# Moving transfers, merging softmax sums and shortening the tail in a two-layer attention kernel

## The chip, the cores and the metric

The kernel runs on one core of a Trainium2 chip. The metric is the device time of one execution in microseconds (us); a kernel is run several times, and medians are quoted with the lowest and highest run beside them. "Span" is the length of the one execution that was profiled; it lies some 2 us below the time of the same run. The *granted clock* is the share of TensorE's full clock that the profile records; in these traces it is 1.00 or 0.5 at any moment, and a stretch can have a mean between. TensorE is called PE in the profile, VectorE is DVE, ScalarE is ACT, GpSimd is POOL, and SP is the engine that issues most of the transfers.

## The reference

Eight images of 64 channels and 64 x 64 pixels go through two attention layers. Both have 4096 tokens per image and a softmax over all of them; layer 0 has 8 channels for f and g, layer 1 has 64 for q and k and a group norm ahead.

```
def layer0(x, Wf, bf, Wg, bg, Wh, bh):
    xf = x.reshape(b, c, n)
    f = einsum('oc,bcn->bon', Wf, xf) + bf
    g = einsum('oc,bcn->bon', Wg, xf) + bg
    hh = einsum('oc,bcn->bon', Wh, xf) + bh
    beta = softmax(einsum('bci,bcj->bij', f, g), axis=2)
    return x + einsum('bcj,bij->bci', hh, beta)

def layer1(x, gamma, beta, w_qkv, b_qkv, w_proj, b_proj):
    xn = group_norm(x, gamma, beta)
    q, k, v = split(einsum('oc,bchw->bohw', w_qkv, xn) + b_qkv)
    attn = softmax(q @ k.T * c ** -0.5)
    out = einsum('oc,bchw->bohw', w_proj, attn @ v) + b_proj
    return out + x
# x: (8, 64, 64, 64) fp32; output = layer1(layer0(x))
```

## The kernel before

The work is cut into 64 *chunks*: 8 images x 2 layers x 4 groups of queries. A chunk has 16 *steps*; in each, PE makes scores, ACT takes the exponential into tiles `e`, PE multiplies these by the values into an accumulator `acc`, and DVE adds the tiles into `esum`, from which the softmax sums come. The order of the layers is L0 of image 0, L0 of image 1, L1 of image 0, L0 of image 2, L1 of image 1, and so on; so L1 of image 6 is chunks 56 to 59 and L1 of image 7 chunks 60 to 63. Work that prepares the next layer or finishes the last chunk hangs in a list with a step number (`at_step`) and is put between the steps when its number is due. A layer's preparation is numbered from the start of a block of 64 steps.

The end of a chunk, with the four narrow products of ones that sum `esum` over the partitions, and a trip through DRAM that spreads the reciprocals over the partitions:

```
        def finish(self, acc, esum, c, index):
            raw = work.tile([P, CW], F32, tag="raw", ...)
            self.total(raw, acc)                       # empties the accumulators
            ...
            def sums(spare):
                ...
                for p in range(2):
                    for h in range(2):
                        matmul(z[ts(2 * h + p, 32), :], ones, esum[:, p, h, :],
                               start=True, stop=True, tile_position=(0, 32 * (2 * h + p)))
                zs = work.tile([P, CW], F32, tag="zs", ...)
                nc.scalar.copy(zs, z)
                for h in range(2):
                    for p in range(2):
                        row = 32 * (2 * h + p)
                        nc.sync.dma_start(zt[ts(h, C), p, :], zs[row : row + 1, :])

            def reciprocals():
                nc.vector.tensor_add(zh, zt[:, 0, :], zt[:, 1, :])
                rt = stash[:, ts(index, QP)]
                nc.vector.reciprocal(rt, zh)
                nc.sync.dma_start(dealt, rt)
                for h in range(2):
                    row = dealt[ts(h, C), :].rearrange("p e -> (p e)")
                    nc.sync.dma_start(r[ts(h, C), :], row.partition_broadcast(C))

            def result():
                nc.vector.tensor_mul(raw, raw, r)
                self.residual(raw, c)
```

Layer 0's preparation: two projections, each of which ends in 16 small transfers that deal f and g to the partitions:

```
            return [(5, begin, True), (8, lambda: self.project(1), True)] + [ ... values ... ]

        def project(self, k):
            ...
            high = work.tile([P, 2, CW], F32R, tag="high", bufs=1, ...)
            ...
            for j in range(2):
                ...   # 8 transfers for each j
                nc.sync.dma_start(dst[rows, cols].bitcast(F32), split[...].bitcast(F32))
```

Layer 1's preparation (group statistics, normalised input, projections), the numbering of a chunk's end, and the last lines: the check of all reciprocals against bounds makes a flag `n_bad`, on which every engine then branches to a general path that is never taken here.

```
            at = [13, 17, 21]
            units = [(at[0], channels, False), (at[1], means, True), (at[2], deviations, True)]
            for c in range(NC):
                s = 30 + 8 * c
                units += [(s - 5, lambda c=c: normal(c), False), ...]
...
            at_step(now + delay, lambda: sums(spare), not spare)
            at_step(now + delay + 2, reciprocals, False)
            at_step(now + delay + 4, result, False)
...
    while later:
        later.pop(0)[2]()
    ok = work.tile(list(stash.shape), F32, tag="zs", name="ok")
    ...                                            # bounds check of all 64 x 8 columns
    nc.vector.tensor_copy(n_bad, ps[0:1, 0, 0:1])
```

## Time and profile before

| | before |
|---|---|
| time, median of the first 3 runs (us) | 3171.41 (3170.2 to 3171.55) |
| span of the profiled run (us) | 3168.3 |
| PE / DVE / ACT busy | 98% / 78% / 65% |
| first exp of the first chunk (us) | 22.40 |
| last accumulation to the end of the span (us) | 18.90 |

How to read it: PE is busy nearly all the time, so only what PE does or waits for can move the time much. The table of waits of the kernel before gives what waited, for what, in total, how often and at the longest (us). The wait that the argument is about is small in it:

```profile
PE acc_l L123 <- DVE raw_l L529: 10.9, 6, 2.3
```

Six waits, one in each of the six chunks in which layer 1's second chunk runs beside the next image's preparation.

In the rest of the document I use one table that is my own working from the traces: the length of each of the 64 chunks, from its first exp instruction to the first of the next (the last one to the end of the span). It adds up to the span together with the *head*, the time before the first exp.

### The profile page before, as it was taken

The page shows a single profiled execution, that of the slowest core. Times are in us where ns is not written, and L with a number is a line of the kernel's source. Part 1 is how long each engine was busy: PE and PEld are TensorE (multiplying, and loading weights), DVE is VectorE, ACT ScalarE, POOL GpSimd, SP SyncE. Part 2 cuts the span into 40 slices and gives each one's busy share as a digit, 9 for nine tenths or more (in the row PEclk, how much of TensorE's full clock was granted, in tenths as well). Part 3 has the DMA queues.
Part 4 walks back from the last instruction along what each step waited for, and adds up shares of the span by engine and source line. Part 5 has one row for each costly group of instructions (what it writes and reads, how often), then busy time and mean ns, then how long its engine had stood idle before and what let it go on. Part 6 is the DMA issues. An engine that isn't in the chain of part 4 may idle for free.

```text
span 3168.3 us, 58576 instructions
## 1 busy us (share of the span) xinstructions
PE 3102.1 (98%) x25525; PEld 1144.6 (36%) x25525; DVE 2467.3 (78%) x1620; ACT 2068.7 (65%) x2225; POOL 16.6 (1%) x41
## 2 busy tenths in 40 slices
PE   7999999999999999999999999999999999999997
PEld 2333334433343333433334333443333433333432
DVE  6999776797768977689776897768977699766675
ACT  5787655786557865578655786557855588555554
POOL 2000000000000000000000000000000000000000
PEclk9999999999999999999999999999999999999999
DMA  4000010100101010010100101001010000000000
GB/s 95 8 8 18 21 28 15 31 8 22 24 15 31 8 29 17 18 28 8 35 11 18 28 8 34 12 18 28 11 31 20 10 18 8 5 21 15 12 11 16
DMA packets 66409, 63.54 MB, mean 20 GB/s; under 512 B 39409, under 2 KB 39489, under 8 KB 66145
## 3 DMA queue, kind: packets, MB, share of 16 engines
q1 hardware_dynamic: 65024, 59.56, 7.8%
q8 instruction: 202, 3.31, 0.4%
q14 instruction: 63, 0.51, 0.1%
q0 software_dynamic: 800, 0.15, 0.0%
q10 hardware_dynamic: 320, 0.01, 0.0%
HBM read 25.33 MB, written 8.65 MB: 11 GB/s over the span
## 4 chain that ended last, share of the span: by engine, by line
PE 86%; DVE 6%; ACT 3%; DMA 2%; SPq 2%; issue 1%; ACTq 0%; DVEq 0%
PE acc_l L123 51%; PE s_l L123 30%; DVE esum_l L602 4%; ACT e_l L630 3%; PE z_l L123 2%; SPq L390 1%; PE qk_l L123 1%; PE v_l L123 1%; DMA r_l<-recips 1%; DVE high_l L380 0%; DMA zt_l<-zs_l 0%; SPq L312 0%; DMA recips<-stash 0%; PE fg_l L123 0%; DMA w<-in_WgT_dram 0%
## 5 line engine op out<-in xcount | busy, mean ns | idle before, releaser
L630 ACT ACTIVATE e_l<-s_l 128x1024 f32<-128x1024 f32 x2048 | 1968.5, 1025 | 1056.2 <-PE s_l L123 1056.2
L602 DVE TENSOR_TENSOR esum_l<-esum_l,e_l 128x2048 f32<-128x2048 f32 x896 | 2050.3, 2288 | 399.6 <-ACT e_l L630 356.8
L123 PE MATMUL acc_l<-e_l,v_l 64*64 64x512 f32 (+1 forms) x8704 | 1126.7, 593 | 10.9 <-DVE raw_l L529 10.9
L123 PE MATMUL s_l<-kq_l 64*64 64x512 f32 (+1 forms) x8448 | 1035.1, 587 | 6.7 <-DVE v_l L282 4.7
L123 PE MATMUL acc_l<-e_l,vt_l 128*64 128x512 f32 x3584 | 838.9, 602 | 0.7
L123 PEld LDWEIGHTS acc_l<-e_l,v_l 64*64 64x64 f32 (+1 forms) x8704 | 384.6, 134 | 578.6 <-issue 516.3
L123 PEld LDWEIGHTS s_l<-kq_l 64*64 64x64 f32 (+1 forms) x8448 | 375.7, 135 | 574.8 <-issue 524.8
L123 PEld LDWEIGHTS acc_l<-e_l,vt_l 128*64 128x64 f32 x3584 | 229.8, 136 | 458.8 <-issue 447.3
L123 PE MATMUL s_l<-fg_l 32*128 32x512 f32 x1792 | 230.8, 469 | 16.0 <-ACT e_l L630 9.8
L123 PEld LDWEIGHTS s_l<-fg_l 32*128 32x128 f32 x1792 | 92.4, 183 | 277.9 <-ACT e_l L630 194.3
L602 DVE TENSOR_TENSOR esum_l<-e_l,e_l 128x2048 f32<-128x2048 f32 x64 | 146.2, 2285 | 47.2 <-ACT e_l L630 47.2
L326 DVE TENSOR_TENSOR raw_l<-raw_l,r_l 128x512 f32<-128x512 f32 x64 | 44.1, 689 | 82.1 <-DMA r_l<-recips 81.9
L316 DVE TENSOR_TENSOR zh_l<-zt_l 128x8 f32<-128x8 f32 x64 | 10.5, 164 | 101.8 <-DMA zt_l<-zs_l 101.8
L123 PE MATMUL z_l<-esum_l,ones 128*32 128x512 f32 x512 | 68.2, 604 | 1.5 <-DVE vt_l L282 1.4
L529 DVE COPY raw_l<-acc_l 128x512 f32<-128x512 f32 x32 | 22.1, 690 | 28.8 <-PE acc_l L123 28.8
L308 ACT COPY zs_l<-z_l 128x512 f32<-128x512 f32 x64 | 38.2, 598 | 5.0 <-PE z_l L123 5.0
L503 ACT ACTIVATE kq_l<-qk_l,qkb 128x512 f32<-128x512 f32 x64 | 40.6, 696 | 0.0
L123 PE MATMUL qk_l<-xn_l,wqk 64*64 64x512 f32 x256 | 33.9, 592 | 0.0
L282 DVE COPY v_l<-v_l 128x512 f32<-128x512 f32 x36 | 24.7, 687 | 6.9 <-PE v_l L123 6.9
L123 PEld LDWEIGHTS v_l<-wh,x 64*64 64x64 f32 x1024 | 22.9, 140 | 14.8 <-issue 13.1
L123 PE MATMUL fg_l<-x,wfg 64*64 64x512 f32 x128 | 18.3, 652 | 9.7 <-DVE low L165 9.7
L123 PEld LDWEIGHTS v_l<-wvp,xn_l 64*64 64x64 f32 x1024 | 21.5, 134 | 16.0 <-issue 14.5
(83 smaller groups left out, 345.2 us busy)
## 6 DMA issues: line engine op xcount, KB each, us to landing
r_l<-recips SPq DMA_DIRECT2D x128, 128.0 KB, 2.9
fg_l<-high_l SPq DMA_DIRECT2D x224, 64.0 KB, 2.0
x<-in_x_dram SPq DMA_DIRECT2D x32, 256.0 KB, 4.8
kq_l<-kq_l SPq DMA_DIRECT2D x64, 128.0 KB, 2.3
out_dram<-raw_l SPq DMA_DIRECT2D x64, 128.0 KB, 2.3
zt_l<-zs_l SPq DMA_DIRECT2D x256, 2.0 KB, 1.8
kq_l<-high_l SPq DMA_DIRECT2D x32, 64.0 KB, 2.0
recips<-stash SPq DMA_DIRECT2D x64, 4.0 KB, 1.4
```

Of the source, the lines that this page charges most:

```text
L123: in_order(nc.tensor.matmul(*args, **kwargs))
L282: self.copy_values(self.vt[:, :, ts(c, TPC), :], ps[:, :, 0 : TPC * C].rearrange("k p (t c) -> k p t c", c=C),)
L308: nc.scalar.copy(zs, z)
L316: nc.vector.tensor_add(zh, zt[:, 0, :], zt[:, 1, :])
L326: nc.vector.tensor_mul(raw, raw, r)
L390: nc.sync.dma_start(dst[rows, cols].bitcast(F32), split[ts(2 * j + i, 32), half, :].bitcast(F32),)
L503: nc.scalar.activation(self.parts[:, h, cols], ps[:, h, :], AF.Identity, bias=k1["qkb"][:, h : h + 1],)
L529: nc.vector.tensor_copy(raw, acc[0])
L602: nc.vector.tensor_add(esum, first if t == 1 else esum, e)
L630: nc.scalar.activation(e[:, p], ps, AF.Exp, scale=at.scale)
```

## The change

Its intent: five things. (1) In layer 1 DVE adds the two halves of `esum`, so the products of ones have 256 columns instead of 512. (2) Work that ends in transfers is numbered so that the 16 f/g transfers and the transfers of the sums do not meet: layer 0's projections go from steps 5 and 8 to 2 and 25, reciprocals come 3 or 4 steps after the sums instead of 2 and results as long again after them, and layer 1's statistics come 3 steps and its normalising 2 steps later. (3) The last chunk takes its reciprocals of the full 128x512 sums straight from PSUM, without the transfers, and its bounds are checked apart. (4) Images 1 and 2 are loaded behind image 0's 32 f/g transfers, and (5) image 1's projections start at steps 12 and 28.

```diff
@@ finish
-            self.total(raw, acc)
+            copied = self.total(raw, acc)
+            width = CW if self.kind == 0 else CW // 2
+            if self.kind == 1:
+                with tc.issue_after(copied.ins):
+                    nc.vector.tensor_add(esum[:, 0], esum[:, 0], esum[:, 1])
 ...
+                        what = esum[:, i, h, :] if self.kind == 0 else esum[:, 0, h, ts(i, width)]
                         matmul(
-                            z[ts(2 * h + p, 32), :], ones, esum[:, p, h, :],
-                            start=True, stop=True, tile_position=(0, 32 * (2 * h + p)),
+                            z[row : row + 32, 0:width], ones[:, 0:32], what,
+                            start=True, stop=True, tile_position=(0, row),
                         )
 ...
+            def at_once():
+                z = ps_s.tile([P, 2, CW], F32, tag="s", name=f"z_{n}")[:, 0, :]
+                for h in range(2):
+                    matmul(z[ts(h, C), :], ones, esum[:, 0, h, :], start=True, stop=True)
+                nc.vector.reciprocal(r, z)
+                result()
+                bounds(r, 1)
 ...
+            if index == 2 * B * NC - 1:
+                return (at_once,)
@@ Layer0.before
-            return [(5, begin, True), (8, lambda: self.project(1), True)] + [
+            at = (12, 28) if self.b == 1 else (2, 25)
+            return [(at[0], begin, True), (at[1], lambda: self.project(1), True)] + [
@@ Layer1.before
-            at = [13, 17, 21]
+            at = [16, 20, 24]
 ...
-                    (s - 5, lambda c=c: normal(c), False),
+                    (s - 3, lambda c=c: normal(c), False),
@@ start
-    for b in (1, 2):
-        load_x(b)
+    with tc.issue_after(layers0[0].sent.ins):
+        for b in (1, 2):
+            load_x(b)
@@ weigh
-            at_step(now + delay + 2, reciprocals, False)
-            at_step(now + delay + 4, result, False)
+            wait = 4 if i + 1 < len(seq) and seq[i + 1][0].kind == 0 else 3
+            at_step(now + delay + wait, reciprocals, False)
+            at_step(now + delay + 2 * wait, result, False)
@@ end
+    bounds(stash, 0)
     while later:
         later.pop(0)[2]()
 ...
-    matmul(ps[0:1, 0, 0:1], bad, ones[:, 0:1], start=True, stop=True)
-    nc.vector.tensor_copy(n_bad, ps[0:1, 0, 0:1])
+    matmul(bad_ps, bad[:, 0:1], ones[:, 0:1], start=True, stop=False)
+    matmul(bad_ps, bad[:, 1:2], ones[:, 0:1], start=False, stop=True)
+    nc.vector.tensor_copy(n_bad, bad_ps)
```

More of the change, by code (lines that the diff above doesn't have):

```diff
@@ L62 @@
     fast_path(tc, n_bad, *args)
-    reg = nc.values_load(n_bad[0:1, 0:1], min_val=0, max_val=P)
+    reg = nc.values_load(n_bad[0:1, 0:1], min_val=0, max_val=2 * P)
     with tc.If(reg > 0):
@@ L178, in fast_path @@
     make_identity(nc, ident)
-    ones = const.tile([P, 32], F32, name="ones")
+    ones = const.tile([P, C], F32, name="ones")
     nc.vector.memset(ones, 1.0)
@@ L198, in fast_path @@
     QP = 2 * CW // P
-    stash = const.tile([P, 2 * B * NC * QP], F32, name="stash")
+    stash = const.tile([P, (2 * B * NC - 1) * QP], F32, name="stash")
     recips = [dram.tile([P, QP], F32, name=f"recips_{i}") for i in range(2 * B * NC)]
@@ L300, in sums @@
                     z = ps_s.tile([P, 2, CW], F32, tag="s", name=f"z_{n}")[:, 0, :]
-                for p in range(2):
-                    for h in range(2):
+                zs = work.tile([P, CW], F32, tag="zs", name=f"zs_{n}")[:, 0:width]
+                for h in range(2):
+                    for i in range(2):
+                        row = 32 * (2 * h + i)
+                        what = esum[:, i, h, :] if self.kind == 0 else esum[:, 0, h, ts(i, width)]
                         matmul(
-                            z[ts(2 * h + p, 32), :], ones, esum[:, p, h, :],
-                            start=True, stop=True, tile_position=(0, 32 * (2 * h + p)),
-                        )
-                zs = work.tile([P, CW], F32, tag="zs", name=f"zs_{n}")
-                nc.scalar.copy(zs, z)
+                            z[row : row + 32, 0:width], ones[:, 0:32], what,
+                            start=True, stop=True, tile_position=(0, row),
+                        )
+                nc.scalar.copy(zs, z[:, 0:width])
                 for h in range(2):
-                    for p in range(2):
-                        row = 32 * (2 * h + p)
-                        nc.sync.dma_start(zt[ts(h, C), p, :], zs[row : row + 1, :])
+                    for i in range(2):
+                        row = 32 * (2 * h + i)
+                        dst = zt[ts(h, C), i, :] if self.kind == 0 else zt[row : row + 32, 0, :]
+                        nc.sync.dma_start(dst, zs[row : row + 1, :])
             def reciprocals():
-                zh = small.tile([P, QP], F32, tag="zh", name=f"zh_{n}")
-                nc.vector.tensor_add(zh, zt[:, 0, :], zt[:, 1, :])
+                zh = zt[:, 0, :]
+                if self.kind == 0:
+                    nc.vector.tensor_add(zh, zh, zt[:, 1, :])
                 rt = stash[:, ts(index, QP)]
@@ L323, in reciprocals @@
                     nc.sync.dma_start(r[ts(h, C), :], row.partition_broadcast(C))
+            def at_once():
+                z = ps_s.tile([P, 2, CW], F32, tag="s", name=f"z_{n}")[:, 0, :]
+                for h in range(2):
+                    matmul(z[ts(h, C), :], ones, esum[:, 0, h, :], start=True, stop=True)
+                nc.vector.reciprocal(r, z)
+                result()
+                bounds(r, 1)
             def result():
@@ L389, in project @@
                         for i, (dst, half) in enumerate(((self.f, h), (self.g, p))):
-                            nc.sync.dma_start(
+                            self.sent = nc.sync.dma_start(
                                 dst[rows, cols].bitcast(F32),
@@ L529, in total @@
             nc.vector.tensor_copy(raw, acc[0])
-            nc.vector.tensor_add(raw, acc[1], raw)
+            return nc.vector.tensor_add(raw, acc[1], raw)
         def residual(self, o, c):
@@ L608, in weigh @@
                 delay = NT
-            sums, reciprocals, result = at.finish(acc, esum, c, i)
+            works = at.finish(acc, esum, c, i)
+            if len(works) == 1:
+                at_step(now, works[0])
+                return
+            sums, reciprocals, result = works
             at_step(now + delay, lambda: sums(spare), not spare)
-            at_step(now + delay + 2, reciprocals, False)
-            at_step(now + delay + 4, result, False)
+            wait = 4 if i + 1 < len(seq) and seq[i + 1][0].kind == 0 else 3
+            at_step(now + delay + wait, reciprocals, False)
+            at_step(now + delay + 2 * wait, result, False)
     for i, (at, c) in enumerate(seq):
@@ L640, in fast_path, with bounds @@
         weigh(*r, len(seq) * NT)
+    bad = const.tile([P, 2], F32, name="bad")
+    bad_ps = ps_a.tile([P, CW], F32, tag="a", name="bad_ps")[0:1, 0:1]
+    def bounds(recip, i):
+        ok = work.tile(list(recip.shape), F32, tag="zs", name=f"ok_{i}")
+        nc.vector.tensor_scalar(ok, recip, 1.0 / SUM_MAX, None, op0=ALU.is_ge)
+        nc.vector.scalar_tensor_tensor(
+            ok, recip, 1.0 / SUM_MIN, ok, op0=ALU.is_le, op1=ALU.mult
+        )
+        least = small.tile([P, 1], F32, tag="least", name=f"least_{i}")
+        nc.vector.tensor_reduce(least, ok, axis=AX.X, op=ALU.min)
+        nc.vector.tensor_scalar(bad[:, i : i + 1], least, -1.0, 1.0, op0=ALU.mult, op1=ALU.add)
+    bounds(stash, 0)
     while later:
         later.pop(0)[2]()
-    ok = work.tile(list(stash.shape), F32, tag="zs", name="ok")
-    nc.vector.tensor_scalar(ok, stash, 1.0 / SUM_MAX, None, op0=ALU.is_ge)
-    nc.vector.scalar_tensor_tensor(ok, stash, 1.0 / SUM_MIN, ok, op0=ALU.is_le, op1=ALU.mult)
-    least = small.tile([P, 1], F32, tag="least", name="least")
-    nc.vector.tensor_reduce(least, ok, axis=AX.X, op=ALU.min)
-    bad = small.tile([P, 1], F32, tag="bad", name="bad")
-    nc.vector.tensor_scalar(bad, least, -1.0, 1.0, op0=ALU.mult, op1=ALU.add)
-    ps = ps_s.tile([P, 2, CW], F32, tag="s", name="bad_ps")
-    matmul(ps[0:1, 0, 0:1], bad, ones[:, 0:1], start=True, stop=True)
-    nc.vector.tensor_copy(n_bad, ps[0:1, 0, 0:1])
+    matmul(bad_ps, bad[:, 0:1], ones[:, 0:1], start=True, stop=False)
+    matmul(bad_ps, bad[:, 1:2], ones[:, 0:1], start=False, stop=True)
+    nc.vector.tensor_copy(n_bad, bad_ps)
 @with_exitstack
```

## The prediction

> **What bounds the kernel now.** I read the page first, for the engines' shares.
>
> ```profile
> PE 3102.1 (98%) x25525; PEld 1144.6 (36%) x25525; DVE 2467.3 (78%) x1620; ACT 2068.7 (65%) x2225; POOL 16.6 (1%) x41
> PEclk9999999999999999999999999999999999999999
> L326 DVE TENSOR_TENSOR raw_l<-raw_l,r_l 128x512 f32<-128x512 f32 x64 | 44.1, 689 | 82.1 <-DMA r_l<-recips 81.9
> L316 DVE TENSOR_TENSOR zh_l<-zt_l 128x8 f32<-128x8 f32 x64 | 10.5, 164 | 101.8 <-DMA zt_l<-zs_l 101.8
> L123 PE MATMUL z_l<-esum_l,ones 128*32 128x512 f32 x512 | 68.2, 604 | 1.5 <-DVE vt_l L282 1.4
> ```
>
> TensorE (PE) is busy 98% of 3168.3 us, at a granted clock above nine tenths. VectorE (DVE) sits 184 us before two instructions, waiting for the transfers that carry the softmax sums (zt) and the reciprocals (r). That is no gain in itself: PE idles only 66 us in all, and 184 us of DVE waiting can cost no more than what of it reaches PE.
>
> So I cut the span into 64 chunks of 32 exp instructions on ACT (one chunk is 512 queries of one image and layer) and compared chunks of the same kind with the view of stretches. The first row is layer 1's second chunk of image 1, beside which the next image's layer 0 is prepared; the second is the same chunk of image 6, with no layer 0 beside it; the third is a bare chunk of the last image.
>
> ```profile
> core 0: us, PE busy (x) PEld busy (x) DVE busy (x) ACT busy (x) POOL busy (x), PEclk, DMA share, GB/s
> 803.36:865.46 62.10, 60.41 (x536) 23.34 (x532) 45.77 (x45) 32.67 (x35) 0.00 (x0) 0.97 0.06 14
> 2747.45:2805.34 57.89, 57.89 (x536) 20.35 (x532) 41.51 (x43) 32.70 (x35) 0.00 (x0) 1.00 0.07 15
> 2980.08:3036.25 56.17, 56.17 (x524) 22.01 (x520) 37.36 (x22) 31.55 (x34) 0.00 (x0) 1.00 0.04 11
> ```
>
> The first two rows have the same 536 PE instructions, yet differ by 4.2 us: 1.7 us idle, the rest slowed matmuls, which count as busy. The timelines of the DMA queue (SP), DVE and PE just before show why:
>
> ```profile
> 768.97 10.67 SPq L390 DMA_DIRECT2D fg_l<-high_l  x16
> 779.74 2.46 SPq L312 DMA_DIRECT2D zt_l<-zs_l  x4
> ```
>
> ```profile
> 783.40 0.17 DVE L316 TENSOR_TENSOR zh_l<-zt_l 128x8 f32<-128x8 f32 x1 [8.63 <-DMA zt_l<-zs_l]
> 792.32 16.60 DVE L602 TENSOR_TENSOR esum_l<-esum_l,e_l 128x2048 f32<-128x2048 f32 x7
> 808.85 0.68 DVE L529 COPY raw_l<-acc_l 128x512 f32<-128x512 f32 x1
> ```
>
> ```profile
> 809.59 3.62 PE L123 MATMUL acc_l<-e_l,v_l 64*64 64x512 f32 x14 [1.69 <-DVE raw_l L529]
> ```
>
> Sixteen f/g transfers hold the queue for 10.67 us, the sums' transfers wait behind them, DVE waits 8.63 us for those, works off seven exp sums in one piece, and empties the accumulators too late, for which PE waits. Against the undisturbed 57.9 us, the six chunks of this kind took 61.94, 62.10, 60.75, 62.00, 61.03 and 60.26: 20.7 us lost together. The chain of waits shows the two ends of the span; at the start the weights land late among x transfers, at the end three transfers in a row stand between the sums and the result:
>
> ```profile
> 2.70 6.46 DMA w<-in_WgT_dram
> ...
> 3153.12 1.79 DMA zt_l<-zs_l
> ...
> 3155.46 1.39 DMA recips<-stash
> ...
> 3157.42 3.29 DMA r_l<-recips
> ```
>
> [...] The trace has only 8-column reciprocals, 203 ns against about 153 ns for one-column one-source operations: 50 ns for 7 columns, or 7 ns a column. It does not contradict a slow reciprocal.
>
> **The change part by part.**
>
> 1. *Merged sums, 256-column products.* In layer 1, for 31 of 32 chunks, DVE adds the halves of esum[...] and loses the 0.16 us add of zh. The ones products keep eight instructions, four at a time, so two rounds: 2 x 0.43 become 2 x 0.21 us. A bare chunk (56.17 us) is 32 blocks of 1.717 us (54.94) plus 1.23 for the product; it should become 55.75. PE is the bound there, so this is on the path: 31 x 0.43 = 13.3 us; I take 12.5[...]. [...] DVE has some 19 us of slack a chunk, behind the emptying of the accumulators, so off the path.
> 2. *Placement.* Layer 0's two projections move from steps 5 and 8 to 2 and 25 of the 64 (a step is 3.4 us in layer 1); sums of the chunk before come at 7, reciprocals 3 or 4 steps later instead of 2. Sixteen issues from step 3 end at about 6, ahead of the sums. The wait of 8.63 us should vanish, and with it most of the 20.7 us; I take 16.5 (80%), since the second projection (2.0 us of DVE) now falls beside the normalising work of steps 24 to 30.
> 3. *Early chunks and image 6.* Chunks 5 to 7, image 1's layer 0 with layer 1's preparation, took 40.2, 45.6 and 42.8 us against 38.0 for a plain one; they hold 3.2 us of PE waiting for a copy of v. The last preparation holds 1.6. I take 3.5 and 1.5: some of it is real work.
> 4. *Images 1, 2 behind f and g.* The last weights wait 6.46 us to land, in a stretch where x transfers of 256 KB land 1.1 us apart; with four of them ahead instead of nine, I take 1.7 us earlier start. Image 1's projections at 12 and 28 also leave the first chunk (45.4 us, 6 above its work) more room: 3 us more with chunks 0 to 2.
> 5. *The end.* From the last accumulation (3149.44) to the end are 18.9 us. After: copy and add 1.45,[...] products of two 64-column halves about 1.1, reciprocal of 128x512 by 7 ns a column 3.6 plus fixed 0.15, product and residual 1.5; then output to the end as now, 6.0 (3162.3 to 3168.3). Sum 15.0, so 3.9 gained. Were the reciprocal as fast as an add, 0.7 us, it would be 7.
>
> Sum: 12.5 + 16.5 + 3.5 + 1.5 + 1.7 + 3 + 3.9 = 42.6 us, so 3171.4 - 42.6 = 3129 us.
>
> **The rivals.**
>
> *The wait moves.* [...] the projection at 25, the deviations at 24, results at 27 and the merge could together delay a copy of v, and PE waits for its buffer. For it: DVE is busiest in this very chunk (45.8 of 62 us)[...]. Against: 58 us of room. It would give back 1 to 2 us an image: about 3140.
>
> *DVE becomes the bound in layer 0.* A plain layer 0 chunk lasts 38.0 us with 36.4 to 36.8 of DVE. For it: margin of about a microsecond. Against: the merge of the last layer 1 chunk falls into layer 0's first chunk, where DVE has 4 us free, and nothing is added to the other three. If it bites, 7 images lose 1 us each.
>
> *The transfers were hidden anyway.* If the 20.7 us came from the order of PE's work rather than the late DVE, placement gives nothing: 3145. Against: equal instructions, 57.9 us where no f/g transfer runs.
>
> *The end gives nothing.* A slow reciprocal on 512 columns, and bounds checks queued ahead of it: 2 to 4 us.
>
> **Range and chances.** All parts at their full size (13.3, 20.7, 8 in the early chunks, 7 at the end) give some 3115; placement failing by half together with a small end gives 3145. What is left is PE work that the change does not touch, so over 2% (below 3108) would need gains that I see nowhere: 6%. Slower by over 2% would need a new stall of 1.6 us in every chunk: 1%.
>
> **What would show it.** The z group with 256 columns for most and about half the duration; bare chunks at about 55.7 us; waits of DVE for zt and r at a third or less of 184 us; PE's wait for raw gone, and the six chunks near 57.5 plus the moved projection (1 us); first exp at about 20.7 instead of 22.4 us; a reciprocal of 3 to 4.5 us at the end and the end some 15 us behind the last accumulation. I would be wrong if a 256-column product cost as much as one of 512 (the switch, not the columns, being its price), if PE waited elsewhere for DVE, or if image 1 came too late at step 12.

Passages that rested on something that no trace or run of this case shows are cut from it; the cuts are marked. The sum came to 42.6 us and 3129 us with all its terms. One term of part 5 went with the cuts, the time of the merge on DVE: the terms that are left there add up to 13.8 us (1.45 + 1.1 + 3.6 + 0.15 + 1.5 + 6.0), while the 15.0 us and the 3.9 us gained have the merge in them. In part 1, what DVE's merges would cost is cut too, and so is the ground for taking 12.5 us instead of 13.3, which was not shown. That 256 columns should take half of 512's 0.43 us was an estimate from that figure.

## The result and the profile after

The changed kernel took 3135.51 us (3133.82 to 3137.1, 5 runs), the kernel before 3171.55 us (3170.2 to 3175.55, 5 runs) on the same chip. All outputs are right. The ratio is 0.9885, with a 95% interval of 0.9872 to 0.9899: faster by 1.15%, which counts as the same at the 2% mark. (A ratio is the mean time of one kernel's fast runs over the mean of the other's from the same rounds, so it is not quite the ratio of the medians.) Predicted were 3129 us and a gain of 42.6 us; measured is a gain of 36.0 us in the medians and of 34.5 us in the spans.

Rows of the page after that answer to those in the prediction (its span is 3133.8 us):

```profile
PE 3082.4 (98%) x25523; PEld 1145.6 (37%) x25523; DVE 2505.2 (80%) x1624; ACT 2061.3 (66%) x2224; POOL 16.5 (1%) x41
L344 DVE TENSOR_TENSOR raw_l<-raw_l,r_l 128x512 f32<-128x512 f32 x64 | 44.1, 689 | 80.0 <-DMA r_l<-recips 79.9
L327 DVE RECIPROCAL stash<-zt_l 128x8 f32<-128x8 f32 x63 | 12.7, 202 | 42.4 <-DMA zt_l<-zs_l 41.4
L296 DVE TENSOR_TENSOR esum_l<-esum_l 128x1024 f32<-128x1024 f32 x32 | 38.9, 1215 | 0.0
```

PE is still the bound at 98%. DVE does more (38.9 us of merging, the last row, 1215 ns each), and it still waits for transfers: 79.9 us for r as before, and 41.4 us for zt, to which 13.0 us before layer 0's remaining add of zt come. That is 134 us, where I had expected a third of 184 us or less.

The groups by form show the narrower products (mean ns is the number behind the busy time):

```profile
L123 PE MATMUL z_l<-esum_l,ones 128*32 128x512 f32 x256 | 34.1, 605 | 0.0
L123 PE MATMUL z_l<-esum_l,ones 128*32 128x256 f32 x248 | 19.8, 391 | 1.3 <-DVE vt_l L282 1.3
L123 PE MATMUL z_l<-esum_l,ones 128*64 128x512 f32 x4 | 2.0, 1081 | 2.8 <-DVE esum_l L296 2.8
```

248 of the products, 8 in each of 31 chunks, now have 256 columns. Their means, 605 and 391 ns, include the time in which four overlap (by the starts in the traces, in a bare chunk the second four begin 0.45 us behind the first with 512 columns, in the kernel before, and 0.24 us with 256, in the kernel after), so the mean fell by a third only; what counts is the chunk.

Stretches of three chunks after, in the columns of the prediction's stretches (length, then busy time and number of instructions of PE, PE weight loads, DVE, ACT and POOL, then granted clock, DMA share and GB/s): layer 1's second chunk of image 1, of image 6, and a bare chunk of image 7.

```profile
795.39:854.03 58.64, 58.64 (x544) 22.32 (x540) 44.19 (x45) 33.56 (x37) 0.00 (x0) 1.00 0.13 33
2716.68:2775.55 58.87, 57.77 (x536) 22.02 (x532) 42.38 (x43) 32.55 (x35) 0.00 (x0) 1.00 0.07 15
2948.22:3003.97 55.75, 55.75 (x524) 22.03 (x520) 38.36 (x22) 31.31 (x34) 0.00 (x0) 1.00 0.04 11
```

The first went from 62.10 to 58.64 us although it took in eight PE instructions, and PE has no gap in it any more; the wait of PE for raw is no longer in the table of waits. The bare one is the predicted 55.75. The second, with no layer 0 near it, grew by about 1 us and has a gap of 1.10 us that was not there.

The timelines of SP and DVE ahead of the first of these chunks show the transfers apart: the 16 f/g transfers are done before the four of the sums are issued.

```profile
751.56 10.43 SPq L412 DMA_DIRECT2D fg_l<-high_l  x16
765.84 2.42 SPq L320 DMA_DIRECT2D zt_l<-zs_l  x4
```

```profile
769.47 0.17 DVE L325 TENSOR_TENSOR zt_l<-zt_l 128x8 f32<-128x8 f32 x1 [1.80 <-DMA zt_l<-zs_l]
...
797.94 0.69 DVE L551 COPY raw_l<-acc_l 128x512 f32<-128x512 f32 x1 [1.71 <-PE acc_l L123]
```

The wait for zt fell from 8.63 to 1.80 us. And at the second line the roles are exchanged: DVE now stands ready and waits 1.71 us for PE's accumulator, where before PE waited 1.69 us for DVE's copy.

By chunks (sums in us, my working from the traces):

| part of the span | before | after | gain | of which merged sums, 0.43 a chunk |
|---|---|---|---|---|
| head, to the first exp | 22.40 | 21.49 | 0.9 | |
| chunks 0 to 2 | 128.67 | 128.77 | -0.1 | |
| chunks 5 to 7 | 128.55 | 127.30 | 1.3 | |
| layer 1, images 0 to 5, first chunks | 348.71 | 343.56 | 5.2 | |
| same, second chunks | 368.07 | 352.49 | 15.6 | 2.6 |
| same, third chunks | 366.30 | 363.66 | 2.6 | 2.6 |
| layer 0, images 2 to 7 (chunks 12 to 55) | 914.20 | 908.91 | 5.3 | 5.2 |
| image 6 (chunks 56 to 59) | 232.87 | 232.21 | 0.7 | 1.3 |
| bare chunks 60 to 62 | 168.50 | 167.22 | 1.3 | 1.3 |
| last chunk with the end | 75.86 | 74.11 | 1.8 | 0.4 |

The rows gain 34.4 us; the spans differ by 34.5. Layer 1's fourth chunks are 338.24 us in both. So merged sums are 13.3 us, placement 5.2 + 15.6 - 2.6 = 18.2 us, and everything else together about 2.8 us, where I had put 13.6.

### The profile page after: what moved, and what is told of

Same layout as the page of the kernel before. It is cut to its first block, busy times and chain, and to the rows that moved or that the text cites. A ratio compares the mean times of both kernels' runs of the same rounds, so it can differ in the third digit from the quotient of the medians.

```text
span 3133.8 us, 58576 instructions
## 1 busy us (share of the span) xinstructions
PE 3082.4 (98%) x25523; PEld 1145.6 (37%) x25523; DVE 2505.2 (80%) x1624; ACT 2061.3 (66%) x2224; POOL 16.5 (1%) x41
## 4 chain that ended last, share of the span: by engine, by line
PE 86%; DVE 6%; ACT 3%; issue 2%; DMA 2%; SPq 1%; ACTq 0%; DVEq 0%
PE acc_l L123 50%; PE s_l L123 32%; DVE esum_l L625 5%; ACT e_l L659 3%; PE z_l L123 1%; PE qk_l L123 1%; PE v_l L123 1%; DMA r_l<-recips 1%; SPq L320 1%; DMA zt_l<-zs_l 0%; PE fg_l L123 0%; DMA recips<-stash 0%; SPq L412 0%; DVE raw_l L344 0%; DMA w<-in_WgT_dram 0%
## 5 line engine op out<-in xcount | busy, mean ns | idle before, releaser
L625 DVE TENSOR_TENSOR esum_l<-esum_l,e_l 128x2048 f32<-128x2048 f32 x896 | 2050.8, 2289 | 388.6 <-ACT e_l L659 346.8
L123 PE MATMUL acc_l<-e_l,v_l 64*64 64x512 f32 (+1 forms) x8704 | 1106.2, 591 | 0.0
L123 PE MATMUL s_l<-kq_l 64*64 64x512 f32 (+1 forms) x8448 | 1019.5, 586 | 5.7 <-ACT e_l L659 3.3
L344 DVE TENSOR_TENSOR raw_l<-raw_l,r_l 128x512 f32<-128x512 f32 x64 | 44.1, 689 | 80.0 <-DMA r_l<-recips 79.9
L123 PE MATMUL z_l<-esum_l,ones 128*32 128x512 f32 (+2 forms) x508 | 55.9, 504 | 4.1 <-DVE esum_l L296 2.8
L327 DVE RECIPROCAL stash<-zt_l 128x8 f32<-128x8 f32 x63 | 12.7, 202 | 42.4 <-DMA zt_l<-zs_l 41.4
L296 DVE TENSOR_TENSOR esum_l<-esum_l 128x1024 f32<-128x1024 f32 x32 | 38.9, 1215 | 0.0
L315 ACT COPY zs_l<-z_l 128x512 f32<-128x512 f32 (+1 forms) x63 | 31.1, 494 | 0.2 <-PE z_l L123 0.2
L123 PEld LDWEIGHTS v_l<-wh,x 64*64 64x64 f32 x1024 | 22.4, 135 | 15.4 <-issue 13.3
```

Source lines behind the costliest of these rows:

```text
L123: in_order(nc.tensor.matmul(*args, **kwargs))
L296: nc.vector.tensor_add(esum[:, 0], esum[:, 0], esum[:, 1])
L315: nc.scalar.copy(zs, z[:, 0:width])
L625: nc.vector.tensor_add(esum, first if t == 1 else esum, e)
```

## The experiments

Eleven kernels ran, in three groups with one chip each. placement_only, delays_only, projects_only and merge_only alter the kernel before; x_early, old_end, no_last_check and high_own, and then no_delays, merge_twice and best, alter the kernel after. The kernel before ran beside each group (3173.55, 3172.38 and 3171.6 us). The questions were: which part of the placement gains; do the parts add up; why do the start and the end give so little; and can what is lost be mended.

### placement_only: the placement on the kernel before

```diff
-            return [(5, begin, True), (8, lambda: self.project(1), True)] + [
+            at = (5, 8) if self.b == 1 else (2, 25)
+            return [(at[0], begin, True), (at[1], lambda: self.project(1), True)] + [
 ...
-            at = [13, 17, 21]
+            at = [16, 20, 24]
-                    (s - 5, lambda c=c: normal(c), False),
+                    (s - 3, lambda c=c: normal(c), False),
-            at_step(now + delay + 2, reciprocals, False)
-            at_step(now + delay + 4, result, False)
+            wait = 4 if i + 1 < len(seq) and seq[i + 1][0].kind == 0 else 3
+            at_step(now + delay + wait, reciprocals, False)
+            at_step(now + delay + 2 * wait, result, False)
```

> The kernel before with the placement alone: layer 0's two projections of images 2 to 7 at steps 2 and 25, layer 1's statistics at 16, 20, 24, normalising 3 steps ahead, reciprocals and results 3 or 4 and 6 or 8 steps after the sums. If the placement is what gave the changed kernel its six second chunks back (18 us by the trace), this is 17 to 19 us faster than before, some 3153 us, with PE's wait for raw gone. If the gain needed the merged sums as well (the freed DVE or PE time), it is under 10 us.

Measured: 3151.07 us (3149.29 to 3153.36), ratio 0.9930 (0.9913 to 0.9946); the span is 3151.7. The first and second chunks of layer 1 went from 716.78 to 698.06 us, a gain of 18.7; all else moved by some 2 us the other way, of which the scatter of the first chunks (128.67 to 131.24) is the most. The placement is a real gain of its own, not something that the other parts bring.

### delays_only and projects_only: its two halves

delays_only is the diff above without its first three lines; projects_only is those three lines alone.

> The placement without the move of the projections: they stay at steps 5 and 8, only the reciprocals, results and layer 1's statistics come later. Theory queue: the sixteen f/g transfers ahead of the sums are the cause, DVE then still waits 3 to 4 us for the sums of the chunk before and the second projection still follows at once; the gain is under half, 4 to 9 us. Rival: DVE merely asked too early, and asking 3 steps later is enough; the gain is the full 17 to 19 us.

> The projections of images 2 to 7 at steps 2 and 25, everything else as before: sums asked for 2 steps after their products. Theory queue: the f/g transfers are out of the way, the wait of 8.6 us falls to the bare round trip (2 to 4 us), and the gain is nearly the full one, 14 to 18 us. Rival: asking too early was the cause; under 6 us.

Measured: delays_only 3175.72 us (3172.57 to 3178.15), ratio 1.0012 (0.9995 to 1.0028); projects_only 3150.39 us (3149.62 to 3151.25), ratio 0.9929 (0.9912 to 0.9945). The whole gain lies in moving the projections. Of the 4 to 9 us that I had expected from the delays alone nothing came, nor did DVE's wait fall to 3 to 4 us. DVE's timeline in the chunk that the prediction showed, with the delays alone:

```profile
784.56 0.17 DVE L316 TENSOR_TENSOR zh_l<-zt_l 128x8 f32<-128x8 f32 x1 [8.56 <-DMA zt_l<-zs_l]
...
793.37 16.61 DVE L602 TENSOR_TENSOR esum_l<-esum_l,e_l 128x2048 f32<-128x2048 f32 x7
809.89 0.68 DVE L529 COPY raw_l<-acc_l 128x512 f32<-128x512 f32 x1
```

The wait, the seven adds in one piece and the late copy are all there as before: the sums' transfers still stand behind f/g's. (projects_only moves the projections' own work on DVE as well, but DVE stood idle for those 8.6 us, so it is the transfers that count.) With the projections moved alone:

```profile
774.93 0.17 DVE L316 TENSOR_TENSOR zh_l<-zt_l 128x8 f32<-128x8 f32 x1 [1.80 <-DMA zt_l<-zs_l]
...
803.40 0.69 DVE L530 COPY raw_l<-acc_l 128x512 f32<-128x512 f32 x1 [1.71 <-PE acc_l L123]
```

The table compares all four of this group (us, my working from the traces):

| | before | placement_only | projects_only | delays_only | merge_only |
|---|---|---|---|---|---|
| layer 1, first chunks x6 | 348.71 | 343.56 | 343.56 | 348.71 | 348.71 |
| layer 1, second chunks x6 | 368.07 | 354.50 | 352.52 | 369.85 | 371.36 |
| chunks 5 to 7 | 128.55 | 128.83 | 129.90 | 127.33 | 129.81 |
| last chunk with the end | 75.86 | 76.67 | 75.96 | 75.77 | 76.70 |

Both chunks with the projections moved alone are 20.7 us shorter: the whole loss that the prediction had worked out, not four fifths of it. The first chunks are 0.86 us shorter each, by the eight PE instructions of the second projection, which the second chunks now hold. The delays on top cost 2.0 us in the second chunks. And the total waiting of DVE stays large while the gain is complete, as the table of waits of projects_only has it:

```profile
DVE raw_l L326 <- DMA r_l<-recips: 86.3, 29, 4.4
DVE zh_l L316 <- DMA zt_l<-zs_l: 61.0, 33, 3.8
```

So the sum of the waits was never the price. It was the single long wait just ahead of the emptying of the accumulators.

### merge_only: the merged sums on the kernel before

All 32 chunks of layer 1 get the merge and the products of 256 columns; nothing moves and the end stays as it was.

```diff
-            self.total(raw, acc)
+            copied = self.total(raw, acc)
+            if self.kind == 1:
+                with tc.issue_after(copied.ins):
+                    nc.vector.tensor_add(esum[:, 0], esum[:, 0], esum[:, 1])
 ...   # and the products, copies and transfers of width 256 as in the change
```

> The kernel before with the merged layer 1 sums and products of 256 columns alone, for all 32 chunks of layer 1. If the products' columns are their price on PE, each chunk is 0.43 us shorter: 13.3 to 13.8 us in all, some 3157.5 us, with bare chunks at 55.74 instead of 56.17 us. If the late DVE of the six second chunks is made worse by 1.2 us more on DVE, 2 to 6 us of it are lost: 3160 to 3164.

Measured: 3165.2 us (3162.7 to 3167.2), ratio 0.9975 (0.9959 to 0.9992), so some 8 us; by the span (3163.6) it is 4.7 us. The 0.43 us a chunk are there wherever nothing else is in play: bare chunks 168.50 to 167.22, layer 0 914.20 to 909.12. But the second chunks of layer 1 became 3.3 us longer instead of 2.6 shorter, and the last chunk 0.8 longer. The table of waits of merge_only names a part of it:

```profile
PE acc_l L123 <- DVE raw_l L538: 13.0, 6, 2.4
```

It is the wait of the kernel before, 10.9 us there. Where DVE is already late at the emptying of the accumulators, 1.2 us more of work ahead of it can make it later still. But of the 5.9 us that these chunks lost against the expected 2.6 us gain, only 2.1 are waiting. In these chunks the granted clock stood at 0.5 for 17.1 us, against 10.2 in the kernel before, which costs some 3.4 us more (half of the difference, an estimate; it takes matmuls to last twice as long at 0.5, and the four products at the end took 1.97 us at 0.5 in the kernel after and 1.08 us at 1.00 in x_early); and delays_only, with 13.3 us of PE idle in them, had only 3.4 us at 0.5. How much of merge_only's loss is the merge's doing, and how much the clock's, is not separated. Either way the parts did not add up in these runs: the merge is worth 13.3 us behind the placement and some 5 to 8 us without it.

### merge_twice: is DVE's added work free in the kernel after?

```diff
                     nc.vector.tensor_add(esum[:, 0], esum[:, 0], esum[:, 1])
+                    if index < 2 * B * NC - 1:
+                        nc.vector.tensor_scalar(esum[:, 1], esum[:, 1], 1.0, None, op0=ALU.mult)
```

> The changed kernel with a second operation over one half of esum right behind the merge (times one, 128x1024, 31 times; the result is the same). Theory: DVE has room in layer 1, its added work is off the path; the time stays within 1.5 us. Rival: DVE's merge is paid; with some 0.6 us each it is 5 us or more slower.

Measured: 3134.15 us (3133.72 to 3134.49), ratio 0.9885 (0.9868 to 0.9901), the same ratio as the kernel after. The added instruction took 0.69 us, 31 times: 21 us more of DVE, and nothing of it in the time. The second chunks of layer 1 are 352.68 us against 352.49. Behind the placement, this much more DVE work in layer 1 is off the path, as the prediction had it.

### no_delays: the kernel after without the later steps

```diff
-            at = [16, 20, 24]
+            at = [13, 17, 21]
-                    (s - 3, lambda c=c: normal(c), False),
+                    (s - 5, lambda c=c: normal(c), False),
-            wait = 4 if i + 1 < len(seq) and seq[i + 1][0].kind == 0 else 3
+            wait = 2
```

> The changed kernel with the old steps for everything but the projections: reciprocals 2 steps after the sums, results 4, layer 1's statistics at 13, 17, 21, normalising 5 ahead. The runs that moved only the projections or only the delays say: the delays shorten chunks 5 to 7 by some 2.6 us, and lengthen the six second chunks of layer 1 by 1.5 to 2 us and chunks 57 and 58 by 1 to 2. Sum about zero: within 2 us of the changed kernel. If the delays carry a share of the gain, it is over 3 us slower.

Measured: 3134.04 us (3133.31 to 3135.07), ratio 0.9886 (0.9869 to 0.9902). The kernel after has 0.9885, so the delays are worth nothing in sum (the span is 2.2 us shorter without them, 3131.6 us, less than the intervals can tell; 0.9 us of it lies in the last chunk, for a reason told under no_last_check). By chunks they give and take: without them the second chunks of layer 1 are 2.5 us shorter (349.96), image 6 is 1.5 us shorter (230.75; the kernels with the delays scatter from 231.24 to 232.52), and chunks 5 to 7 are 1.3 us longer (128.60). The loss in image 6 can be seen in the kernel after, in the timelines of DVE and PE in its second chunk:

```profile
2746.56 0.69 DVE L344 TENSOR_TENSOR raw_l<-raw_l,r_l 128x512 f32<-128x512 f32 x1 [3.74 <-DMA r_l<-recips]
```

```profile
2750.36 1.09 PE L123 MATMUL s_l<-kq_l 64*64 64x512 f32 x8 [1.10 <-DVE ve_l L474]
```

DVE waits 3.74 us for the reciprocals of the chunk before; the deviations' small work (ve) is queued behind that on DVE, and the buffer that it reads is one that PE's scores need next. The prediction's rival "the wait moves" is this, at a small scale: the later steps put the deviations behind the wait for r.

### x_early: the start without the new order of loads

```diff
-            at = (12, 28) if self.b == 1 else (2, 25)
+            at = (5, 8) if self.b == 1 else (2, 25)
 ...
-    with tc.issue_after(layers0[0].sent.ins):
-        for b in (1, 2):
-            load_x(b)
+    for b in (1, 2):
+        load_x(b)
```

> The changed kernel with images 1 and 2 loaded as before (right behind image 0) and image 1's projections back at steps 5 and 8. If the order of the transfers is worth what the prediction put on it (1.7 us of start and 3 us in the first three chunks), this is 3 to 5 us slower than the changed kernel. Rival: what the start gained is given back in the first chunk, whose second half waits for the second projection either way; under 1.5 us slower.

Measured: 3136.21 us (3135.13 to 3139.47), ratio 0.9889 (0.9872 to 0.9905), where the kernel after has 0.9885. The head is 21.61 us against 21.49, chunks 0 to 2 are 129.06 against 128.77: the new order is worth nothing that these runs can see. The 0.9 us of head that the kernel after seemed to gain come from elsewhere: PE's first instruction came at 9.68 us in the one profiled run of the kernel before, at 9.03 in the kernel after, and at 8.97 in placement_only, which has the start of the kernel before letter for letter. The last of the first weights landed at 9.16 us in the kernel before and at 8.66 us in the kernel after, so 0.50 of the 0.65 us between these two are its landing.

### high_own: what holds the first chunk

In the kernel after PE waits twice in the first chunk for f/g transfers (0.53 us, shown, and 0.64 us a little later), and then its granted clock goes down to 0.5 (from 43.2 to 46.6 us), so that twelve accumulating instructions take 4.49 us, where the usual twelve take 2.80:

```profile
41.26 0.56 PE L123 MATMUL s_l<-fg_l 32*128 32x512 f32 x2 [0.53 <-DMA fg_l<-high_l]
...
42.89 4.49 PE L123 MATMUL acc_l<-e_l,vt_l 128*64 128x512 f32 x12
```

The two projections of image 0 share the buffer `high`, so the second cannot fill it until the first one's 16 transfers have read it. The experiment gives the second its own place, in a buffer that is free at the start.

```diff
-            high = work.tile([P, 2, CW], F32R, tag="high", bufs=1, name=f"high_{n}")
+            if self.b == 0 and k == 1:
+                high = work.tile([P, 2, 2, CW], F32R, tag="esum", name=f"high_{n}")[:, 0]
+            else:
+                high = work.tile([P, 2, CW], F32R, tag="high", bufs=1, name=f"high_{n}")
```

> The changed kernel, with a buffer of its own for the second projection of image 0 (a slot of the exp sums' pool that is free then), so that it need not wait until the first projection's sixteen transfers have landed. Theory: PE's waits of 0.5 and 0.6 us for f/g at 41 us, and the slow matmuls behind them at a lower clock, come from this; the first chunk is 2 to 3 us shorter. Rival: the transfers' own issue time (0.63 us each, thirty-two in a row) is the limit, the first chunk stays at 43 to 44 us.

Measured: 3132.15 us (3131.56 to 3133.04), ratio 0.9872 (0.9855 to 0.9888). The first chunk went from 43.94 to 40.52 us. The same 8 us as a stretch, first in the kernel after, then in high_own (columns as above):

```profile
38.00:46.00 8.00, 6.83 (x26) 2.10 (x24) 7.58 (x5) 5.30 (x6) 0.00 (x0) 0.82 0.40 97
```

```profile
38.00:46.00 8.00, 8.00 (x42) 2.54 (x44) 7.69 (x4) 6.94 (x8) 0.00 (x0) 1.00 0.94 216
```

PE gets 42 instructions done instead of 26, at the full clock. The last of image 0's f/g transfers landed at 36.3 us instead of 48.3. (The DMA engines' 94% instead of 40% are the x loads of images 1 and 2, which stand behind those transfers: they are issued from 34.9 us here, from 47.0 us in the kernel after.) So, with this order of loads, the start was held by one buffer. Whether the order counts once the buffer is there, no run tests. Chunks 0 to 2 together took 128.2 to 129.7 us in the six kernels of the after kind without this buffer, and 125.3 and 125.6 us in the two with it (high_own and best). Single chunks are less steady at the start: in the five kernels that share the start of the kernel before, chunk 0 took 45.4 to 48.2 us. From the kernel after to high_own, PE's idle time in the first chunk fell from 2.1 to 1.2 us, and the time at a granted clock of 0.5 from 11.5 to 8.7 us, which is worth some 1.4 of the 3.4 us (half of the difference, an estimate). Between different starts the clock doesn't order the chunks: the kernel before, with 45.4 us, had only 6.3 us at 0.5.

### old_end: the end of the kernel before on the kernel after

```diff
-            if index == 2 * B * NC - 1:
-                return (at_once,)
 ...
-    bounds(stash, 0)
     while later:
         later.pop(0)[2]()
+    bounds(stash, 0)
+    nc.vector.memset(bad[:, 1:2], 0.0)
```

> The changed kernel with its last chunk finished as all others, by three transfers in a row, and the bounds checked in one piece. By the traces the last chunk took 76.70 us in the merge-only run and 74.11 us in the changed kernel: 2.6 us slower. If the prediction's 3.9 us against the old end were right, counting the merge that the old end would now have too, 4.7 us slower.

Measured: 3137.39 us (3135.07 to 3139.49), ratio 0.9888 (0.9872 to 0.9905); the last chunk with the end is 76.95 us against 74.11, so the new end is worth 2.8 us by these traces and some 2 us by the medians. (x_early and no_delays have the new end too and took 73.2 us; see below.) Beside the kernel before (75.86) the old end is 1.1 us longer with merged sums, for the merge (1.21 us in the kernel after) stands ahead of the products here and has nothing to hide behind: in the kernel after, PE waits 2.80 us, until it is done.

### no_last_check: the new end without the check of its own bounds

DVE's timeline of the last microseconds of the kernel after:

```profile
3121.05 3.36 DVE L339 RECIPROCAL r_l<-z_l 128x512 f32<-128x512 f32 x1 [2.16 <-PE z_l L123]
...
3125.38 0.74 DVE L555 SCALAR_TENSOR_TENSOR raw_l<-raw_l,pb,x 128x512 f32<-128x512 f32 x1
...
3127.92 0.14 DVE L690 CAST n_bad<-bad_ps 1x1 int32<-1x1 f32 x1 [0.28 <-PE bad_ps L123]
```

The result is ready at 3126.1 and the flag at 3128.1, 1.9 us later, and the end comes 5.7 us behind the flag. In the kernel before the order was the other way round:

```profile
3157.90 0.15 DVE L654 CAST n_bad<-bad_ps 1x1 int32<-1x1 f32 x1 [0.37 <-PE bad_ps L123]
...
3161.53 0.75 DVE L533 SCALAR_TENSOR_TENSOR raw_l<-raw_l,pb,x 128x512 f32<-128x512 f32 x1
```

The experiment takes the last chunk's bounds check away; its outputs are right, but it no longer guards the last eight columns.

```diff
                 result()
-                bounds(r, 1)
 ...
     bounds(stash, 0)
+    nc.vector.memset(bad[:, 1:2], 0.0)
```

> The changed kernel without the bounds check on the last chunk's reciprocals (its count is set to zero; the result is the same for these inputs). Theory flag: the end waits for the flag, which comes 1.9 us behind the residual and is followed by 5.7 us of branching and draining; without the check the end follows the output instead and is 2 to 2.7 us earlier, at about 2.0 us behind the landing of the last output. Rival: the output transfer sets the end; no change.

Measured: 3133.26 us (3132.8 to 3134.28), ratio 0.9876 (0.9859 to 0.9892). DVE's end now:

```profile
3125.19 0.08 DVE L690 CAST n_bad<-bad_ps 1x1 int32<-1x1 f32 x1
...
3126.04 0.75 DVE L554 SCALAR_TENSOR_TENSOR raw_l<-raw_l,pb,x 128x512 f32<-128x512 f32 x1
```

The flag is out ahead of the result, the end follows the landing of the last output (3130.7) by 1.9 us, and from the last accumulation to the end are 15.5 us instead of 17.6. With the check the end follows the flag, without it the output: the check of 512 columns (0.42, 0.68, 0.69 and 0.15 us, and the product) is on the path in the kernel after.

Ahead of the reciprocal, the last four products took 2.0 us, where the prediction had 1.1. The stretch of 2 us that holds them and the two first products for the flag, in the kernel after and then in x_early, shows why:

```profile
3119.00:3121.00 2.00, 1.97 (x6) 0.39 (x6) 0.00 (x0) 0.00 (x0) 0.00 (x0) 0.50 0.00 0
```

```profile
3119.00:3121.00 2.00, 1.20 (x6) 0.31 (x6) 0.74 (x2) 0.00 (x0) 0.00 (x0) 1.00 0.00 0
```

At a granted clock of 0.50 the four products take 1.97 us, at 1.00 they take 1.08; both times they run two at a time. In the kernel after, high_own, merge_twice, no_last_check and best the clock had fallen before them, 2.2 to 2.8 us behind the last accumulation; in x_early and no_delays it fell only after them, 5.1 to 5.2 us behind it. That is 0.9 us of the last chunk (73.2 instead of 74.1 to 74.3 us), so ends should be compared at the same clock. The kernel after and no_last_check have the same. What sets the moment, no run here shows.

What the 5.7 us behind the flag are: in the trace of the kernel after, ACT and DVE load the flag in 0.48 and 0.55 us, branch, and have their next instruction 3.6 and 3.9 us after the branch (POOL, with the same branch, 0.4 us after it); the closing takes another 1.1 us. Eight packets of the two instruction queues fall into the last 14 us of that trace; what fills the gap, no run here shows.

### best: what the experiments point to

high_own's buffer, the deviations at step 22 instead of 24, and a bounds check of the last chunk on 8 columns: eight further products with `esum` as the stationary operand and one column of ones give the sums dealt over the partitions, as the others' are.

```diff
+                z8 = ps_a.tile([P, CW], F32, tag="a", name="z8")[:, 0:QP]
+                for h in range(2):
+                    for j in range(TPC):
+                        k = h * TPC + j
+                        matmul(z8[:, k : k + 1], esum[:, 0, h, ts(j, P)], ones[:, 0:1], start=True, stop=True)
                 nc.vector.reciprocal(r, z)
+                r8 = small.tile([P, QP], F32, tag="r8", bufs=1, name="r8")
+                nc.vector.reciprocal(r8, z8)
+                bounds(r8, 1)
                 result()
-                bounds(r, 1)
 ...
-            at = [16, 20, 24]
+            at = [16, 20, 22]
 ...   # and high_own's diff
```

> The changed kernel with three mends: a buffer of its own for image 0's second projection (3.4 us in the first chunk by its own run), layer 1's deviations at step 22 instead of 24, ahead of DVE's wait for the reciprocals (up to 0.3 us in each of six chunks and 1.1 us in chunk 57, PE's waits for ve), and the last bounds check on 8 columns of sums instead of 512 of reciprocals (1.5 to 2 us at the end). Together 5 to 7 us faster than the changed kernel, 3128 to 3131 us. If the mends collide, 3 to 4.

Measured: 3127.76 us (3126.5 to 3128.72), ratio 0.9863 (0.9847 to 0.9880). It is faster than the kernel before by 1.4%, and its slowest run is below the fastest of the kernel after (3133.82; that one ran apart from it, beside a kernel before of 3171.55 us, where best had one of 3171.6). By chunks against the kernel after: chunk 0 40.74 against 43.94 us, second chunks of layer 1 350.42 against 352.49, image 6 230.76 against 232.21, last chunk 73.33 against 74.11 (both with the clock at 0.5 in the last four products). At the end the flag comes out 0.9 us behind the result, not 1.9, as DVE's timeline of best shows:

```profile
3119.33 0.75 DVE L565 SCALAR_TENSOR_TENSOR raw_l<-raw_l,pb,x 128x512 f32<-128x512 f32 x1
...
3120.83 0.14 DVE L700 CAST n_bad<-bad_ps 1x1 int32<-1x1 f32 x1 [0.28 <-PE bad_ps L123]
```

The small checks were put between the multiplication and the residual and behind it, so the flag still sets the end. An order that puts them ahead might give another 0.9 us, an estimate that no run tests.

## Why the prediction was right or wrong

**The bound and the class** were right: PE was the bound at 98% and still is, and the gain is of the expected size. 3135.5 us lies between the 3115 and 3145 us that the prediction names as its ends, 6.5 us above the predicted 3129. One of its sums does not come out: placement failing by half (8.3 us) and an end that gives 2 us instead of 3.9 leave 3139 us; 3145 is what placement failing altogether gives.

**Step 1, merged sums, was right in size.** The bare chunk is the predicted 55.75 us, and 31 x 0.43 = 13.3 us are in the trace, where I had taken 12.5. The ground for it is in the trace before: 16 products of 512 columns in 1.72 us, four at a time, so 0.43 us for each four; with half the columns they took about half (0.24 us from four to four where it had been 0.45, and the bare chunk with its eight is 0.43 us shorter). The merge took 1215 ns for 128x1024, where DVE's 128x512 multiplication takes 689 ns and its 128x2048 add 2289 ns. "Off the path" for DVE's added work holds in the changed kernel (merge_twice), which is behind the placement. Without it, merge_only kept 4.7 us of span and some 8 by the medians; how much of the rest DVE took, and how much the clock, is open. I had added the parts up as if they were independent, which happened to do no harm because both are in the change: that was luck.

**Step 2, placement, was right in cause and a little low:** 18.2 us for 16.5. That one transfer queue held up one wait, and that wait the copy, is shown by delays_only and projects_only. What the sums' transfers waited for was SP's issuing, not the landing: an f/g transfer of 64 KB took SP 0.59 us to issue and landed 2.0 us after its issue began (medians), sixteen in a row held SP for 10.4 to 10.8 us, and in the kernel before the first transfer of the sums was issued 0.1 us behind the last of them. Three details of the step were wrong. All of the loss came back, not 80%: the second projection costs at step 25 the 0.86 us that it had cost in the first chunk, and no more. The later reciprocals, which I counted as part of the mechanism, give nothing. And DVE's waits for zt and r fell to 134 us only, not to a third of 184: I had rightly said that their sum is no gain in itself, and then expected them to go anyway. And "slowed matmuls" was left without a cause. Of the 20.7 us, 10.9 are PE's waiting; some 5.1 are the clock (3.41 us at 0.5 in each of three chunks, an estimate), which is why these took 61.9 to 62.1 us and the others 60.3 to 61.0. The last 0.8 us a chunk were not followed. So in one chunk a wait of 1.5 us cost 4.0 (61.94 against 57.9).

**Step 3 was mis-sized.** The early chunks gave 1.3 of 3.5 us, and image 6 lost 0.6 us where I expected a gain of 1.5 (with its merged sums it gained 0.7). Chunk 6 alone gained 4.3 us (45.59 to 41.34): the wait for the copy of v, 3.16 us, went, and with it 3.41 us at a clock of 0.5. But chunk 5 lost 3.0 (40.17 to 43.18), and it was no work that moved: PE has 218 and 268 instructions in these two chunks before and after. A new wait of 2.08 us came, ahead of layer 1's first projection at 262.70 us, whose normalised input DVE had written at 262.55. So this, too, is "the wait moves". In image 6 the delays made a new wait of 1.10 us (no_delays).

**Step 4 was wrong.** I expected 4.7 us from the order of the loads and found 0.8, and x_early shows that even those are not its doing. I had read a wait for the weights from the chain of waits of one run, and took its length for something that the x loads set; the first instruction comes at 9 us with either order, and 9.68 was the outlier. What held the first chunk was the shared buffer, which I did not look for; high_own got 3.4 us there.

**Step 5 was right in the parts that it summed and wrong in the last.** The reciprocal took 3.36 us for an estimated 3.75: 202 ns for 8 columns and 3358 ns for 512 from PSUM are 6.3 ns a column ((3358 - 202) / 504), where I had 7. Two terms were off. The products with 64 columns took 2.0 us, not 1.1; that was the clock of this one run, for at a clock of 1.00 they took the 1.1 us (x_early and no_delays). And "then output to the end as now, 6.0" failed: what the end follows is the later of output and flag, and the change moved the flag behind the result. From the result to the end are 7.7 us instead of 6.0. With both, 15.0 becomes 17.6 us, and the gain 1.3 of 3.9 (16.7 us and 2.2 in the two runs with the clock at 1.00). The last term is the one that failed.

**The sum:** predicted 12.5 + 16.5 + 3.5 + 1.5 + 1.7 + 3 + 3.9 = 42.6; measured 13.3 + 18.2 + 1.3 - 0.6 + 0.9 - 0.1 + 1.3 = 34.3, against 34.5 us of span. The two large terms were 2.5 us too low together, the five small ones 10.8 us too high.

**The rivals.** "The wait moves" came true for about 4 us in all (2.5 in the second chunks and 1.5 in image 6, by no_delays), of which 1.3 us in the early chunks pay back a part (net of the new wait in chunk 5). "DVE becomes the bound in layer 0" did not: its chunks became 5.3 us shorter, as much as the merged sums alone explain. "The transfers were hidden anyway" is refuted by projects_only. "The end gives nothing" was half right, but for the flag, not for a slow reciprocal.

**What stays open:** what fills the 3.6 to 3.9 us between the branch and the next instruction of ACT and DVE, what sets the moment at which the clock falls (at the end, and behind a wait), and whether the order of the loads counts once the second buffer is there.

## What to carry to other kernels

Many microseconds of an engine's waiting can be worth nothing and one wait of 8 us worth three, so follow the single wait that stands ahead of the release of a buffer to the bounding engine, and move what blocks its transfer rather than the one who waits. Before believing a small gain at the start of a kernel, look at how that start varies among runs in which it was not changed. And when a tail is shortened, list everything that the end waits for, flags and branches too, because the second-latest takes over. And look at the granted clock before you explain a slow matmul by anything else: here the same four products took 1.08 us at 1.00 and 1.97 us at 0.5.
